# Cross-attention softmax weights: turned by VectorE in 32x32 squares and moved by transfers inside SBUF, with seven products chained in PSUM and divisions on GpSimd

## The chip, the cores and the metric

The kernel runs on one core of one Trainium2 chip. The metric is the device time of one execution in microseconds; the median of three runs of the kernel before is 2532.26 us (2529.63 to 2534.01). A core has TensorE (matmuls; PE, with its weight loads as PEld), VectorE (DVE), ScalarE (ACT), GpSimd (POOL) and SyncE (SP), each with its own in-order instruction stream, and 16 DMA engines. All data here is float32. SBUF is the working memory with 128 partitions; PSUM takes the results of TensorE, in 8 banks of 2 KB a partition.

## The reference

The reference is a cross-attention block (L0) followed by a transformer block (L1) of a diffusion model: self-attention, a second cross-attention on the same context, and an MLP. B = 8, N = 512 tokens, H = 512, 16 heads of 32, context S = 77. The change touches the two cross-attentions only. Cut to these:

```python
# L0: cross-attention with adaptive LayerNorm; lq = 512, lkv = 77
xq  = _ada_ln(x_q,  t_vec, Wss_q,  bss_q)
xkv = _ada_ln(x_kv, t_vec, Wss_kv, bss_kv)
q = (xq @ Wq + bq).reshape(B, Lq, nh, dh)
kv = (xkv @ Wkv + bkv).reshape(B, Lkv, 2, nh, dh)
scores = jnp.einsum('bqhd,bkhd->bhqk', q, k) / jnp.sqrt(jnp.float32(dh))
attn = jax.nn.softmax(scores, axis=-1)
out = jnp.einsum('bhqk,bkhd->bqhd', attn, v).reshape(B, Lq, H)
x = x_q + (out @ Wp + bp)
...
# L1, between self-attention and MLP
q_c  = _ln(x) @ W_qc + b_qc
kv_c = _ln(context) @ W_kvc + b_kvc
c_attn_w = jax.nn.softmax(jnp.einsum('bhqd,bhsd->bhqs', q_c, k_c) * scale, axis=-1)
c_attn_out = jnp.einsum('bhqs,bhsd->bhqd', c_attn_w, v_c)
x = x + (c_attn_out @ W_cproj + b_cproj)
```

## The kernel before

The program runs four phases one after another: a cross phase `x` (L0), a self-attention phase `a`, a cross phase `c`, and the MLP phase `m`. Rows of x stay in DRAM between the phases; each phase loads one batch element b at a time (`next_x`, 1 MB a load) and adds its results to the rows in DRAM by accumulating transfers on GpSimd's queue (L664).

A cross phase is `cross_phase`, run twice. Its loop has 32 steps: for every b the 16 heads go in four softmax groups fc of four heads. In the cross phases the order of the work on TensorE, VectorE, ScalarE and GpSimd is the order in which the program lists it; SyncE's order is left to a scheduler. Of one group:

- `scores` (L687): 32 matmuls, four heads by four row tiles of 128 tokens, into two PSUM tiles of two banks (`s`, two buffers, so one group's worth). Half 0 holds heads 0 and 1, half 1 heads 2 and 3.
- Half 0: VectorE takes the row maxima (L703) and writes the differences to SBUF (L704), ScalarE the exponentials in one instruction (L714). Half 1: VectorE takes the negative maxima (L710), and ScalarE computes the exponentials from PSUM in eight instructions of 77 columns with the maximum as bias (L717). VectorE sums both halves (L724), takes reciprocals (L727) and multiplies (L728). The division of half 1 is done one group later, among the next group's maxima.
- `turn` and `keep` (L741, L745): one group later, TensorE turns the weights, four 128x77 squares for each head, into a PSUM tile (tag `t`, two buffers), and ScalarE copies them to SBUF as `pT`, head by head.
- `outputs` (L751, L759): four matmuls with the values, 512 tokens wide, into a `t` tile, copied by ScalarE with the value bias to `oT`.

The order of tokens in `pT` and `oT` is plain. Between the pieces of a group stands other work (`g`, `turned`, `scaled`, `stats`):

- `Seven` (L509): the projections of 512x512 by 512x512 in seven products of half-size blocks, two halves of the output at a time. Each product is two matmuls of 256 columns. The products are written to halves of PSUM banks (tag `m`, two buffers), and their sums are formed on VectorE (L517, L520, L528, L532, and L635 or L670/L671), ScalarE (L631, L634, L659) and GpSimd (L523, L527, L660). `queries` uses it for q of the next b, `project` for the output projection of the b before. The combinations of operands that the products need are formed on GpSimd ahead: `x_sums` (L563 to L566) and `o_sums` (L556 to L559), four instructions of 128x512 each.
- `ln_rows`: LayerNorm statistics (L258, L259), the reciprocal root in small VectorE steps (L220 to L229) and the normalisation of four row tiles on ScalarE (L247). `ln_T`: the normalised rows turned by TensorE (L280) and copied by ScalarE (L284), once a b.
- `fill`: other work in fixed groups (`mod.block`, keys of the context).

Of the kernel before, what the change touches and what calls it, by code (L numbers as in the profile page):

```python
# [11 lines left out]
F32 = mybir.dt.float32  # L12
# [17 lines left out]
def tile_pixart_block(ctx: ExitStack, tc: tile.TileContext, a: dict, out: bass.AP):  # L30
# [241 lines left out]
    def ln_T(b, nm, pool, psp, res, scale=None, shift=None, tag="t"):  # L272
# [4 lines left out]
        for k in range(KC):  # L277
            pt = psp.tile([P, H], F32, tag=tag, name=f"lnT_ps_{nm}{b}_{k}")
            for t in range(NT):
                nc.tensor.transpose(pt[:, ts(t, P)], xb[:, t, ts(k, P)], ident)  # L280
            if scale is None:
                nc.scalar.copy(xT[:, k, :], pt)
            else:
                nc.scalar.activation(  # L284
                    xT[:, k, :], pt, AF.Identity,
                    bias=shift[:, k, b : b + 1], scale=scale[:, k, b : b + 1],
                )
            yield
# [49 lines left out]
    with tc.tile_pool(name="ps_s", bufs=2, space=PSUM, reuse_waits="tile") as ps_s:  # L338
# [147 lines left out]
        class Seven:  # L486
# [5 lines left out]
            ORDER = (1, 2, 6, 5, 7, 4, 3)  # L492

            def __init__(self, nm, lhs, rhs, work, first, fifth, third, dst, done=None):
                self.nm, self.lhs, self.rhs, self.work = nm, lhs, rhs, work
                self.first, self.fifth, self.third = first, fifth, third
                self.dst, self.done = dst, done

            def temp(self, tag):
                return self.work.tile([P, N2], F32, tag=tag, bufs=1 + (tag != "u3"), name=f"{tag}_{self.nm}")  # L500

            def steps(self):
                add = ALU.add
                for n, i in enumerate(self.ORDER):
                    if n % 2 == 0:
                        bank = ps_m.tile([P, 2, N2], F32, tag="m", name=f"s{n}_ps_{self.nm}")
                    ps = bank[:, n % 2]
                    for k in range(2):
                        nc.tensor.matmul(  # L509
                            ps, lhsT=self.lhs[i][:, k], rhs=self.rhs[i][:, k],  # L510
                            start=(k == 0), stop=(k == 1),
                        )

                    if i == 2:
                        p1 = self.temp("p1")
                        self.first(p1, bank[:, 0])
                        nc.vector.tensor_tensor(self.dst[0, 0], ps, p1, add)  # L517
                    elif i == 5:
                        u2, p5 = self.temp("u2"), self.temp("p5")
                        nc.vector.tensor_tensor(u2, bank[:, 0], p1, add)  # L520
                        self.fifth(p5, ps)
                        u4 = self.temp("u4")
                        nc.gpsimd.tensor_tensor(u4, u2, p5, add)  # L523
                    elif i == 4:
                        u3 = self.temp("u3")
                        self.third(u3, bank[:, 0], u2)
                        nc.gpsimd.tensor_tensor(self.dst[1, 1], u3, p5, add)  # L527
                        nc.vector.tensor_tensor(self.dst[1, 0], ps, u3, add)  # L528
                        if self.done is not None:
                            self.done(1)  # L530
                    elif i == 3:
                        nc.vector.tensor_tensor(self.dst[0, 1], ps, u4, add)  # L532
                        if self.done is not None:
                            self.done(0)
                    yield

        def cross_phase(
# [11 lines left out]
            add, sub = ALU.add, ALU.subtract  # L549

# [3 lines left out]
            def sums(engine, s1, s2, s3, s4, a11, a12, a21, a22):  # L554

                engine.tensor_tensor(s1, a21, a22, add)  # L556
                engine.tensor_tensor(s2, s1, a11, sub)
                engine.tensor_tensor(s3, a11, a21, sub)
                engine.tensor_tensor(s4, a12, s2, sub)  # L559

            def differences(engine, t1, t2, t3, t4, b11, b12, b21, b22):

                engine.tensor_tensor(t1, b12, b11, sub)  # L563
                engine.tensor_tensor(t2, b22, t1, sub)
                engine.tensor_tensor(t3, b22, b12, sub)
                engine.tensor_tensor(t4, b21, t2, sub)  # L566
# [4 lines left out]
            sums(  # L571
                nc.gpsimd, *sq,
                w_q[:, low, :H2], w_q[:, high, :H2], w_q[:, low, H2:], w_q[:, high, H2:],
            )
            to = four("to", [P, 2, H2])

            dq = small.tile([P, 2], F32, tag="dq", bufs=1, name=f"dq_{nm}")
            nc.vector.tensor_tensor(dq, bias_cols(bq, 2, 2), bias_cols(bq, 2, 0), sub)


            db = work.tile([P, H2], F32, tag="db", bufs=1, name=f"db_{nm}")
            nc.gpsimd.tensor_tensor(db, bo_row[:, H2:], bo_row[:, :H2], sub)

            def weights_o():
                differences(
                    nc.gpsimd, *to,
                    w_o[:, low, :H2], w_o[:, low, H2:], w_o[:, high, :H2], w_o[:, high, H2:],
                )

            def x_sums(b, engine):  # L590
# [4 lines left out]
                differences(  # L595
# [4 lines left out]
            def o_sums(b, engine):  # L600
# [4 lines left out]
                sums(  # L605
# [4 lines left out]
            def queries(b, j):  # L610
# [7 lines left out]
                for i in range(2):  # L618
# [8 lines left out]
                }  # L627
                return Seven(
                    f"q{nm}{b}_{j}", lhs, rhs, work,

                    lambda p1, ps: nc.scalar.activation(  # L631
                        p1, ps, AF.Identity, bias=bias_cols(bq, 1, j)
                    ),
                    lambda p5, ps: nc.scalar.copy(p5, ps),  # L634
                    lambda u3, ps, u2: nc.vector.scalar_tensor_tensor(  # L635
                        u3, ps, dq[:, j : j + 1], u2, add, add
                    ),
                    {(r, c): qT[r][:, (first, second)[c]] for r in range(2) for c in range(2)},
                ).steps()

            def project(b, j):
# [16 lines left out]
                def fifth(p5, ps):  # L658
                    nc.scalar.copy(p5, ps)  # L659
                    nc.gpsimd.tensor_tensor(p5, p5, db, add)  # L660

                def done(r):
# [6 lines left out]
                    f"o{nm}{b}_{j}", lhs, rhs, work,  # L669
                    lambda p1, ps: nc.vector.tensor_tensor(p1, ps, bo_row[:, :H2], add), fifth,  # L670
                    lambda u3, ps, u2: nc.vector.tensor_tensor(u3, ps, u2, add),  # L671
                    {(r, c): res[j + 2 * r][:, ts(c, H2)] for r in range(2) for c in range(2)}, done,
                ).steps()

            class Softmax:


                def __init__(self, b, fc):
                    self.b, self.fc, self.nm = b, fc, f"{nm}{b}_{fc}"

                def scores(self, before):
# [3 lines left out]
                    for t in range(NT):  # L685
# [12 lines left out]
                    self.p = [  # L698
                        work.tile([P, 2, NT, S], F32, tag="p", bufs=4, name=f"p_{self.nm}_{i}")
                        for i in range(2)  # L700
                    ]

                    nc.vector.tensor_reduce(self.mx[0], self.sv[0], AX.X, ALU.max)  # L703
                    nc.vector.tensor_tensor(  # L704
                        self.p[0], self.sv[0], self.mx[0].unsqueeze(3).to_broadcast([P, 2, NT, S]),
                        ALU.subtract,
                    )
                    if before:
                        before.divide(1)
                    nc.vector.tensor_reduce(self.mx[1], self.sv[1], AX.X, ALU.max, negate=True)  # L710

                def exp(self, i, r=0):
                    if i == 0:
                        nc.scalar.activation(self.p[0], self.p[0], AF.Exp)  # L714
                        return
                    for t in range(NT):
                        nc.scalar.activation(  # L717
                            self.p[i][:, r, t, :], self.sv[i][:, r, t, :], AF.Exp,
# [907 lines left out]
```

## Time and profile before

| | |
|---|---|
| median of three runs | 2532.26 us (2529.63 to 2534.01) |
| profiled execution, its span | 2534.4 us |
| cross phase x, first query products to last projections | about 75 to 449 us |
| cross phase c | about 1360 to 1720 us |
| mean granted TensorE clock | 0.988 |
| SyncE transfers of 1 MB for x, per b of a cross phase | one load, in phase x also one DRAM-to-DRAM copy |

The profiled execution's span is 2.1 us above the median of the runs and inside 0.4 us of their highest. In a line of stretches the columns are: the stretch, its length, busy us (and instructions) of PE, PEld, DVE, ACT and POOL, the granted TensorE clock as a share of full speed, the busy share of the DMA engines, and GB/s. In a line of the chain or of the timeline: start in us, length in us, engine, source line, operation or tile, and number of instructions. In a line of groups: line, engine, operation, tiles out<-in, shapes, count, then busy us and mean ns of one, then idle us of the engine just before and what ended it.

### The profile page before, as it was taken

What the parts mean: (1) busy time and instruction counts of PE and PEld (TensorE: products, weight loads), DVE (VectorE), ACT (ScalarE), POOL (GpSimd) and SP (SyncE); (2) the same over time, 40 slices, a digit from 0 to 9 for tenths busy, and PEclk for the clock granted to TensorE, in tenths of its full rate; (3) what the DMA queues carried; (4) which work ended last, traced back from release to release, by engine and by line L of the source; (5) the groups of instructions that cost most, each with busy time, mean ns of one, the idle gap of its engine ahead of it and who ended that gap; (6) DMA issues with size and microseconds to landing.
All of it is one profiled execution on the core that took longest, in us unless ns stands there. A gap on an engine that the chain in (4) does not pass through costs nothing.

```text
span 2534.4 us, 35276 instructions
## 1 busy us (share of the span) xinstructions
PE 2433.2 (96%) x13205; PEld 1561.7 (62%) x13205; DVE 1776.2 (70%) x3230; ACT 1226.2 (48%) x2083; POOL 1087.0 (43%) x982
## 2 busy tenths in 40 slices
PE   7999999889999999999989999998999999999998
PEld 3577776423333333333335777767888888888887
DVE  3588887478889888887756888877556555555553
ACT  1466665377677777777653666662121121121120
POOL 2245452266767777767663454535102102012011
PEclk9899999999999999999999999999999999999999
DMA  7323313498989999999996223133111111001010
GB/s 261 137 51 92 92 26 76 90 180 168 199 171 197 191 181 186 182 188 180 201 200 173 68 39 63 19 81 82 40 32 38 33 39 38 26 29 55 17 38 25
DMA packets 112068, 265.05 MB, mean 105 GB/s; under 512 B 12210, under 2 KB 28674, under 8 KB 111770
## 3 DMA queue, kind: packets, MB, share of 16 engines
q0 software_dynamic: 50976, 159.45, 35.1%
q1 hardware_dynamic: 54981, 91.59, 10.9%
q10 hardware_dynamic: 5941, 11.76, 1.4%
q8 instruction: 104, 1.70, 0.3%
q14 instruction: 66, 0.54, 0.1%
HBM read 226.39 MB, written 44.76 MB: 107 GB/s over the span
## 4 chain that ended last, share of the span: by engine, by line
PE 41%; issue 28%; DVE 15%; DMA 6%; POOL 6%; ACT 3%; POOLq 0%; SPq 0%; ACTq 0%; DVEq 0%
PE s_ps_qx L509 4%; PE s_ps_qc L509 4%; DMA e_a<-mxd_a 4%; DVE mx_a L1005 3%; PE proj_ps_a L301 3%; PE sT_a L985 3%; PE v_ps L301 3%; PE s_ps_ox L509 2%; PE q_ps_a L293 2%; PE s_ps_oc L509 2%; POOL res_m L1535 2%; DVE tu_a L1016 2%; DVE part_a L1017 2%; POOL xr L1536 2%; PE o_ps_a L1065 2%
## 5 line engine op out<-in xcount | busy, mean ns | idle before, releaser
L1535 POOL TENSOR_TENSOR res_m<-res_m,gate_m 128x256 f32<-128x256 f32 x64 | 52.1, 814 | 665.1 <-DVE res_m L1533 665.1
L1039 POOL DMA_DIRECT2D e_a<-mxd_a x256 | 249.8, 2045 | 157.4 <-DMA mxd_a<-mxT_a 138.6
L1048 ACT ACTIVATE e_a<-e_a 128x1024 f32<-128x1024 f32 x256 | 264.8, 1057 | 82.4 <-DMA e_a<-mxd_a 82.2
L1003 ACT COPY e_a<-sT_a 128x1024 f32<-128x1024 f32 x256 | 254.7, 1010 | 100.7 <-DVE mx_a L1005 50.5
L1469 ACT ACTIVATE hT<-hT,bcol 128x512 f32<-128x512 f32 x128 | 91.9, 721 | 237.0 <-DVE hT L1444 228.9
L1055 POOL TENSOR_TENSOR sum_a<-e_a,e_a 128x1024 f32<-128x1024 f32 x64 | 151.0, 2389 | 105.6 <-ACT e_a L1048 105.2
L1055 POOL TENSOR_TENSOR sum_a<-sum_a,e_a 128x1024 f32<-128x1024 f32 x64 | 170.7, 2678 | 3.7 <-ACT e_a L1048 3.6
L1005 DVE TENSOR_TENSOR mx_a<-sT_a,mx_a 128x1024 f32<-128x1024 f32 x128 | 150.8, 1216 | 29.7 <-PE sT_a L985 27.3
L985 PE MATMUL sT_a<-qT_a,kT_a 32*128 32x512 f32 x1024 | 151.6, 646 | 14.0 <-ACT e_a L1003 12.4
L1065 PE MATMUL o_ps_a<-e_a,v 128*32 128x512 f32 x1024 | 146.5, 613 | 9.7 <-ACT e_a L1048 9.7
L1436 PE MATMUL q_ps_h<-x_m,w_L_xcond_W_mlp 128*128 128x256 f32 x512 | 132.1, 381 | 0.0
L1436 PE MATMUL q_ps_h<-xT_m,w_L_xcond_W_mlp 128*128 128x256 f32 x512 | 131.4, 379 | 0.0
L1083 DVE RECIPROCAL rz_a<-z_ps_a 128x512 f32<-128x512 f32 x32 | 107.4, 3357 | 32.0 <-PE z_ps_a L1076 32.0
L293 PE MATMUL q_ps_a<-xnT_a,w_L_xcond_W_qkv 128*128 128x512 f32 x256 | 124.1, 613 | 5.9 <-ACT xnT_a L908 5.9
L1436 PE MATMUL q_ps_h<-x_m,w_s 128*128 128x256 f32 x512 | 122.3, 382 | 5.6 <-DVE w_s L1390 4.9
L293 PE MATMUL k_ps_a<-xnT_a,w_L_xcond_W_qkv 128*128 128x512 f32 x256 | 120.5, 608 | 0.0
L301 PE MATMUL v_ps<-w_L_xcond_W_qkv,xnT_a 128*128 128x512 f32 x256 | 119.7, 611 | 0.0
L301 PE MATMUL proj_ps_a<-w_L_xcond_W_proj,oT_a 128*128 128x512 f32 x256 | 117.9, 604 | 1.4 <-DVE oT_a L1086 1.4
L1436 PE MATMUL q_ps_y<-w_L_xcond_W_mlp,h_s 128*128 128x256 f32 x512 | 113.1, 379 | 0.0
L1436 PE MATMUL q_ps_y<-w_L_xcond_W_mlp,hT 128*128 128x256 f32 x512 | 113.1, 379 | 0.0
L1451 ACT COPY p_h<-q_ps_h 128x256 f32<-128x256 f32 x64 | 23.7, 370 | 183.7 <-PE q_ps_h L1436 183.7
L985 PEld LDWEIGHTS sT_a<-qT_a,kT_a 32*128 32x128 f32 x1024 | 42.0, 183 | 114.4 <-issue 43.4
(368 smaller groups left out, 5609.4 us busy)
## 6 DMA issues: line engine op xcount, KB each, us to landing
e_a<-mxd_a POOLq DMA_DIRECT2D x256, 512.0 KB, 11.7
xa<-res_x POOLq DMA_DIRECT2D x32, 256.0 KB, 5.4
xa<-res_a POOLq DMA_DIRECT2D x32, 256.0 KB, 14.8
x_c<-xa SPq DMA_DIRECT2D x8, 1024.0 KB
w_L_xcond_W_mlp<-in_L_xcond_W_mlp_dram SPq DMA_DIRECT2D x8, 1024.0 KB
xa<-res_c POOLq DMA_DIRECT2D x32, 256.0 KB, 5.2
x_m<-xa SPq DMA_DIRECT2D x8, 1024.0 KB
xr<-xa SPq DMA_DIRECT2D x64, 128.0 KB
```

The costliest lines, as they stand in the source:

```text
L293: nc.tensor.matmul(ps, lhsT=w[:, k, ts(j, P)], rhs=xT[k], start=(k == 0), stop=(k == KC - 1))
L301: nc.tensor.matmul(ps, lhsT=xT[k][:, cols], rhs=w[:, k, :], start=(k == 0), stop=(k == KC - 1))
L509: nc.tensor.matmul(ps, lhsT=self.lhs[i][:, k], rhs=self.rhs[i][:, k], start=(k == 0), stop=(k == 1),)
L985: nc.tensor.matmul(sc[h // 2][:, h % 2, :], lhsT=kT[ts(h, HD), ts(k, P)], rhs=qT[ts(h, HD), :], start=True, stop=True,)
L1003: nc.scalar.copy(self.e[k][i], sc[i])
L1005: nc.vector.tensor_tensor(self.mx[1 - i], sc[1 - i], self.e[0][1 - i] if k == 1 else self.mx[1 - i], ALU.max,)
L1039: nc.gpsimd.dma_start(out=self.e[k][i].rearrange("p h n -> p (h n)"), in_=self.mxd[2 * i : 2 * i + 2, :] .rearrange("h n -> (h n)").partit ...
L1048: nc.scalar.activation(self.e[k][i], self.e[k][i], AF.Exp)
L1055: engine.tensor_tensor(sum_i, self.e[0][i] if k == 1 else sum_i, self.e[k][i], ALU.add)
L1065: nc.tensor.matmul(self.po[ts(h, HD), :], lhsT=vt[:, self.fc * P + h * HD : self.fc * P + (h + 1) * HD], rhs=self.e[k][h // 2][:, h % 2, : ...
L1083: nc.vector.reciprocal(r, self.pz)
L1436: nc.tensor.matmul(self.banks[n][:, half], lhsT=lhsT, rhs=rhs, start=(k == 0), stop=(k == len(pairs) - 1),)
```

## The change

Only `cross_phase`, `Seven` and the PSUM pools change, apart from one buffer count in `ln_T`.

- The weights of a half lie in a fixed buffer `p_half[i]` of 8 blocks of 96 columns (77 and 19 zeros, set once); `pw` and `pT` have one buffer each. VectorE turns them in 32x32 squares (`turn`, one instruction a half), and twelve transfers on SyncE's queue (`send`) move rows of 2 KB between partitions: 32 partitions for each of four query squares and three key squares, 13 in the last. `pT` then holds tokens in another order, which `outputs` undoes in the view that its copy reads. The last group of a phase is still turned by TensorE (`turn_here`).
- The division of both halves runs on GpSimd. The exponentials of half 1 also sum their rows (`accum_out`), so VectorE sums half 0 only.
- The seven products of `Seven` are chained: 1, 6, 5 and 3 accumulate in one PSUM tile, read after each step (`take`); 2 in half of a second, 7 and 4 accumulate in its other half. Products 3 and 4 and what follows them are done in the next group (`pending`). The sums need three additions on VectorE; biases come in with the readings on ScalarE, or on VectorE and GpSimd for projections (`later`, `flush`).
- PSUM tag `m` gets three buffers, tag `t` one.
- `x_sums` and `o_sums` are given out in pieces; row transposes of the next b move from fc = 2 to fc = 0, queries from fc = 3, 0 to fc = 1, 3, projections to fc = 2 and 0, fills by one group or more, the load of x from fc = 3 to fc = 1.

```diff
-            ORDER = (1, 2, 6, 5, 7, 4, 3)
...
+            def mm(self, i):
+                if i == 1:
+                    self.a = ps_m.tile([P, N2], F32, tag="m", name=f"sa_ps_{self.nm}")
+                elif i == 2:
+                    self.b = ps_m.tile([P, 2, N2], F32, tag="m", name=f"sb_ps_{self.nm}")
+                if i in (2, 7):
+                    self.product(self.b[:, i == 7], i, first=True)
+                elif i == 4:
+                    self.product(self.b[:, 1], i)
+                else:
+                    self.product(self.a, i, first=(i == 1))
...
+            def add(self, dst, half, src):
+                nc.vector.tensor_tensor(dst, self.b[:, half], src, ALU.add)
...
+            p_half = [
+                work.tile([P, 2 * NT, KB * SQ], F32, tag=f"half{i}", bufs=1, name=f"p{i}_{nm}")
+                for i in range(2)
+            ]
+            for p in p_half:
+                nc.gpsimd.memset(p[:, :, S:], 0.0)
...
+                def taken(what, dst, ps):
+                    row = j if what in ("p1", "c12") else j + 2
+                    nc.scalar.activation(dst, ps, AF.Identity, bias=bias_cols(bq, 1, row))
...
+                def taken(what, dst, ps):
+                    bias = bo_row[:, H2:] if what in ("u4", "c12") else bo_row[:, :H2]
+                    if what in ("p1", "c12"):
+                        nc.vector.tensor_tensor(dst, ps, bias, add)
+                    else:
+                        nc.scalar.copy(dst, ps)
+                        later.append(lambda: nc.gpsimd.tensor_tensor(dst, dst, bias, add))
...
                     for t in range(NT):
                         nc.scalar.activation(
-                            self.p[i][:, r, t, :], self.sv[i][:, r, t, :], AF.Exp,
-                            bias=self.mx[i][:, r, t : t + 1],
+                            v[:, r, t, :], self.sv[i][:, r, t, :], AF.Exp,
+                            bias=self.mx[i][:, r, t : t + 1], accum_out=self.sm[i][:, r, t : t + 1],
                         )
...
                 def divide(self, i):
-                    nc.vector.reciprocal(self.sm, self.sm)
-                    return nc.vector.tensor_tensor(
-                        self.p[i], self.p[i], self.sm.unsqueeze(3).to_broadcast([P, 2, NT, S]), ALU.mult
+                    v = self.value(i)
+                    nc.gpsimd.tensor_tensor(
+                        v, v, self.sm[i].unsqueeze(3).to_broadcast([P, 2, NT, S]), ALU.mult
                     )
...
+                def turn(self, i):
+                    if i == 0:
+                        self.pw = work.tile([P, KB, 4, NT * SQ], F32, tag="pw", bufs=1, name=f"pw_{self.nm}")
+                    to_ = self.pw[:, :, 2 * i : 2 * i + 2, :].rearrange("p k r (t c) -> p (r t) k c", c=SQ)
+                    nc.vector.transpose(to_, self.p[i].rearrange("p g (k c) -> p g k c", c=SQ))
...
+                def send(self):
+                    self.room()
+                    for i in range(QB):
+                        for k in range(KB):
+                            n = min(SQ, S - k * SQ)
+                            nc.sync.dma_start(
+                                out=self.pT[k * SQ : k * SQ + n, i],
+                                in_=self.pw[i * SQ : i * SQ + n, k],
+                            )
```

The order inside a group becomes (whole, but for the end of a phase and the first group):

```diff
+                now.scores()
+                if before:
+                    before.turn(1)
+                    before.send()
+                if pending:
+                    pending.c22()
+                now.maxima(0)
+                now.shift()
+                now.maxima(1)
+                pump(side, 3)
+                if pending:
+                    pending.mm(3)
+                    pending.take("c12")
+                now.exp(0)
+                if pending:
+                    pending.mm(4)
+                    pending.c21()
+                    pending.stores()
+                run(tail)
+                mm(1)
+                if n:
+                    pump(turned)
+                mm(2)
+                if seven:
+                    seven.take("p1")
+                now.exp(1, 0)
+                now.total(0)
+                now.divide(0)
+                run(side)
+                if n:
+                    pump(turned)
+                mm(6)
+                if n:
+                    pump(turned)
+                mm(7)
+                if fc < 3:
+                    pump(stats)
+                if seven:
+                    seven.take("u2")
+                if n:
+                    pump(turned)
+                mm(5)
+                if seven:
+                    seven.c11()
+                now.exp(1, 1)
+                last = now.total(1)
+                now.divide(1)
+                if seven:
+                    seven.take("u4")
+                flush()
+                if fc == 2:
+                    pump(stats)
+                elif fc == 3:
+                    pump(stats, 2)
+                if n + 1 < B * KC:
+                    now.turn(0)
...
+                if before:
+                    before.outputs()
```

Here `turned` is `ln_T` of the next b (fc = 0), `tail` the last two row normalisations for it, `stats` the LayerNorm pieces of the b after, and `side` the x sums (fc = 1) or o sums (fc = 2).

## The prediction

> **What bounds the kernel now.** I read the page first, then the busy time in equal stretches of both cross phases, then the chain of waits inside one stretch, then the groups of instructions and SyncE's queue in order of time.
>
> ```profile
> PE 2433.2 (96%) x13205; PEld 1561.7 (62%) x13205; DVE 1776.2 (70%) x3230; ACT 1226.2 (48%) x2083; POOL 1087.0 (43%) x982
> ...
> 218.00:261.00 43.00, 42.36 (x354) 33.50 (x353) 37.19 (x80) 28.42 (x71) 21.27 (x22) 1.00 0.32 75
> ```
>
> The second line is one whole batch element b of the first cross phase (from 75 to 449 us; the second runs from 1360 to about 1720): TensorE is busy 42.4 of 43 us at full clock, VectorE 37.2, ScalarE 28.4, GpSimd 21.3. The chain of waits in that stretch is TensorE alone, one softmax group from its scores to the next scores:
>
> ```profile
> 259.09 1.06 PE s_x L687 x32
> 260.15 0.59 PE pT_ps_x L741 x4
> 260.74 1.73 PE s_ps_qx L509 x8
> 262.47 0.44 PE pT_ps_x L741 x4
> ...
> 263.77 0.44 PE pT_ps_x L741 x4
> ...
> 265.08 0.44 PE pT_ps_x L741 x4
> 265.51 2.59 PE s_ps_qx L509 x12
> 268.11 1.00 PE o_ps_x L751 x8
> ```
>
> The group takes 10.0 us: scores 1.06, seven products 6.04, outputs 1.0, and the four turns of weights (pT) 1.9. Scores of b = 3 start at 216.19, of b = 4 at 259.09, of b = 5 at 301.99: 42.9 us per b, three groups near 10.2 and one with the row transposes (lnT) of 12.4.
>
> **What is removed.** The four pT turns: by the timeline 0.50 + 3 x 0.44 = 1.82 us of TensorE a group, 31 groups a phase, two phases: 113 us. Were TensorE still the bound, b would fall to 42.9 - 4 x 1.82 = 35.6 us. ScalarE loses four pT copies a group (L745, 582 ns, starting some 0.49 apart), VectorE two divisions (L728, 851 ns), one sum (L724, 784 ns) and part of the additions behind the products (five or six become three for queries and five for projections, 0.41 to 0.48 each); GpSimd loses the additions L523 and L527 (0.73 each). None of these engines sets the end now.
>
> **What is added.** The rows that I price by:
>
> ```profile
> L717 ACT ACTIVATE p_x<-s_x,mx_x 128x77 f32<-128x77 f32 x256 | 61.7, 327 | 0.4
> L383 POOL TENSOR_TENSOR cT_x<-cT_x,mod_kv 128x616 f32<-128x616 f32 x4 | 4.8, 1213 | 24.6 <-DVE cT_x L379 24.6
> L1016 DVE STREAM_TRANSPOSE tu_a<-mx_a 128x512 f32<-128x512 f32 x128 | 90.7, 708 | 3.3
> ```
>
> - Two GpSimd divisions a group, same shape and broadcast as L383: 1.21 us each. Dear end: GpSimd's slope from 128x256 (725 ns) to 128x512 (1267) carried on to 616 elements, 1.49. I take L383.
> - Two VectorE turns of 768 elements: L1016's 708 ns less some 0.17 fixed (a 128x4 operation takes 0.16), over 512 elements, gives 1.05 ns an element: 0.98 us.
> - Twelve SBUF transfers on SyncE. Four loads issued in a row, and a load that waits for a store to land, show the price:
>
> ```profile
> 1733.97 1.79 SPq L1524 DMA_DIRECT2D xr<-xa  x4
> ...
> 2510.61 0.34 SPq L1537 DMA_DIRECT2D out_dram<-xr  x1
> 2512.33 0.32 SPq L1524 DMA_DIRECT2D xr<-xa  x1
> ```
>
>   Issues are (1.79 - 0.34)/3 = 0.48 us apart, and 1.72 us pass from the start of an issue to the landing. Twelve: 11 x 0.48 + 1.72 = 7.0 us. Cheap end: 0.33 each, 5.4.
> - The eight exponentials of the second half now also sum their rows, and in the changed program each waits for the one before. Today four take 0.96 us (started 0.21 apart). One after another: 0.327 + 0.04 for the hop = 0.37. No row shows the accumulator's own cost: between nothing and a small instruction such as the 128x8 reciprocal (0.20). I take 0.42, 1.7 us for four; ends 0.96 (waits free) and 2.3.
> - Reordered outputs: same element count as L751 and L759 (0.69); taken as nothing, since they run beside the exponentials' chain below; a copy twice as long would add 0.7 us to ScalarE, which is free between u4 and the next first exponential for longer than that. Two memsets of 8x19 at the start (a 128x10 one took 0.13) lie before the first group. Moved fills are the same instructions elsewhere. The products' new waits (each reading of the chained bank ends before the next product) are in the chain below; a product takes 0.87 us, a reading 0.37 to 0.47 and a hop, so one product between covers it.
>
> **The new chain.** This decides. Half buffers p, pw and pT are single, and VectorE's order is reciprocal of half 1, turn 0, turn 1 (waits for GpSimd's division), then c22 and the next maxima. Behind the waiting turn 1 stands the whole next softmax; ScalarE's exponentials wait for it. With time from the end of a turn 1, a query group (fc = 3): c22 0.34, maximum 0.83, shift 0.80, hop 0.05, first exponential 0.61, p1 0.37 (starts 0.61 and 0.37 apart, as L714 and L631 now), = 3.0; four exponentials to 4.7, u2 to 5.0, four more to 6.7; hops and reciprocal 0.4; division 1.21 to 8.3; hop and turn 1.1: **9.4 us**. Beside it: transfers landed at 7.1, outputs 8.1, next scores 9.2, just before the maximum needs them at 9.7; and the next turns, which wait for pw to be free, could end at 7.1 + 2 x 0.98 = 9.05. So TensorE (8.1 us) waits.
>
> The others, by the same rows:
> - fc = 0: after the first exponential (2.63) ScalarE does two row normalisations (L247, 1.5 for two), and its copies xnT (L284, 0.78) stand between the exponentials; tag t has one buffer, so a turn and its copy alternate. Normalised 4.2, turned 4.65, xnT0 5.4, exponentials 7.0, xnT1 7.75, turn and xnT2 9.2, u2 9.5, xnT3 10.7, exponentials 12.3, then 0.4 + 1.21 + 1.1: **15.0**.
> - fc = 1: GpSimd is later. From -1.1: two additions 1.45, three x sums 3.8, two store issues (L664, 1.04) 2.1, division 1.2, fourth sum 1.3, division 1.2, = 9.95; turn: **11.0**.
> - fc = 2: no p1 on ScalarE, exponentials end 6.4, reciprocal 6.7, then seven rsqrt steps (0.2 each, and L228 waits 0.28 longer than its neighbours, twice) to 8.7, two turns: **10.6**.
>
> Sum 46.0 a b against 42.9: +3.1. Twelve full b, and the first and last b of each phase together as two: 14 x 3.1 = 43. The closing turn, which stays on TensorE with one t buffer and a GpSimd division, adds about 1.5 a phase. 43 + 3 = 46 on the span of 2534.4, whose profiled execution lies 2.1 above the median 2532.3; 2532.3 + 46 = **2578**.
>
> [...] L383 takes 1.4 times VectorE's L728. [...] I keep the row. [...]
>
> ```profile
> 90.00:120.00 30.00, 27.83 (x160) 12.85 (x160) 21.59 (x53) 17.13 (x42) 3.16 (x4) 0.77 0.20 63
> ```
>
> Here, where TensorE waits for VectorE between groups, its granted clock is 0.77, against 1.00 in the full stretches. The chain above has it idle a fifth of the time. [...] By the row, outputs and scores at half clock end 2.06 later, 1.5 beyond their slack; in half the groups that is 3 us a b, 42 in all. I take none and keep it as the dear end.
>
> **Rivals.**
> - Cheap ends: accumulators free (0.96), issues 0.33. fc = 3 then 8.2 (TensorE), fc = 0 13.5, fc = 1 stays 11.0 on GpSimd, fc = 2 9.1: 41.8, so 14 x -1.1 + 3 = -12: 2520. For it: the exponentials run 0.21 apart today. Against: the added waits. 0.13.
> - TensorE stays the bound everywhere: -113 + 3: 2422. For it: 98% busy now. Against: fc = 0 and the single buffers. 0.07.
> - Dear ends: accumulators 0.57 apart (+1.2 a group where ScalarE leads), divisions 1.49 (+0.27, twice in fc = 1): 16.5 + 11.5 + 12.1 + 10.9 = 51.0: +8.1 x 14 + 3 = +116: 2648; or the clock, +42 on the forecast. 0.20.
> - A load ahead of the transfers on SyncE (a 1 MB load and a 1 MB copy keep DMA busy 5 us from 204 to 209 us): landing at 12.1, turns at 14 for 11.0 in fc = 1: +3 for 7 b, 21. It lies inside the range; the load waits for lnT3 (about 10) and should be through before turn 1 at 15.
>
> **How the numbers follow.** Forecast 0.60 at 2578, its own range 2545 to 2615. What a measurement can tell is 0.2%, 5 us. Faster: 0.07 and 0.11 of the cheap case, 0.18; same: the rest of it and a sliver of the forecast, 0.05; slower 0.77. The range leaves out the TensorE case and the upper part of the dear one: 2515 to 2645.
>
> **What would show it.** The changed profile should have TensorE near 80% busy in the cross stretches at 46 us per b; exponentials 0.4 apart, not 0.21; GpSimd divisions near 1.2 us; VectorE idle before turn 1 on GpSimd; the fc = 0 group near 15 us. I am wrong if TensorE is still 95% busy there, if accumulating exponentials overlap, or if turn 0 waits on DMA for longer than turn 1 on GpSimd.

## The result and the profile after

The changed kernel takes 2791.22 us (median of 4 runs, 2785.63 to 2794.27), the kernel before 2533.14 in the same comparison: ratio 1.1015, 95% interval 1.0992 to 1.1037. It is slower by 258 us where I forecast slower by 46. The profiled execution has a span of 2787.3 us. First the line of busy time of the changed kernel's page, then its busy time in one stretch of 58 us, which is one b of the first cross phase (columns as in the stretch shown of before: length, TensorE, weight loads, VectorE, ScalarE, GpSimd, granted clock, DMA share, GB/s):

```profile
PE 2470.7 (89%) x12213; PEld 1542.4 (55%) x12213; DVE 1734.7 (62%) x3064; ACT 1193.3 (43%) x2443; POOL 1162.9 (42%) x1016
```

```profile
376.00:434.00 58.00, 45.48 (x300) 32.53 (x300) 35.40 (x70) 26.02 (x93) 25.86 (x24) 0.82 0.31 62
```

A b takes about 58 us, not 42.9 and not the 46.0 of my sum. No engine is full: TensorE is busy 45 of 58, and that at a granted clock of 0.82. So the time is in waits, and in work that runs at a lower clock behind them. The order of time of one group, from the end of a turn to the end of the next, shows which (changed kernel; start, length, engine, instruction, in brackets the idle time before it and what ended it). The first line is SyncE's first send of the group, the next two its third and its last:

```profile
391.54 0.51 SPq L806 DMA_DIRECT2D pT_x<-pw_x  x1
...
392.74 0.80 SPq L806 DMA_DIRECT2D pT_x<-pw_x  x1
...
399.03 1.03 SPq L806 DMA_DIRECT2D pT_x<-pw_x  x1
...
403.05 1.84 DVE L795 STREAM_TRANSPOSE pw_x<-p_x 128x768 f32<-128x768 f32 x2 [4.67 <-DMA pT_x<-pw_x]
403.08 1.94 PE L828 MATMUL o_ps_x<-pT_x,cv_x 77*32 77x512 f32 x8 [4.95 <-DMA pT_x<-pw_x]
404.95 2.01 PE L741 MATMUL s_x<-ckT_x,qT_x 32*128 32x77 f32 x32
...
406.99 0.80 DVE L760 TENSOR_REDUCE mx_x<-s_x 128x8 f32<-128x616 f32 x1 [1.80 <-PE s_x L741]
```

This is a group fc = 1. From the first send to the landing of the last pass 11.5 us, where I had 7.0. VectorE's next turns and TensorE's outputs both wait for that, and the scores stand behind the outputs. TensorE, 4.95 us idle, runs outputs and scores at half speed (1.94 and 2.01 us, against 1.07 and 1.13 when it comes straight from other work), so that the next maximum starts 15.5 us after the first send. My sum had it wanted at 9.7 in a group fc = 3, and by the same steps at some 11.3 in a group fc = 1 (11.0 and the addition c22, 0.34). In the first phase VectorE's turns wait for the landing in 13 of 31 groups, 37.2 us in all, in the second in 16, 48.5 us.

Group by group, from the end of one turn 1 to that of the next (in the changed kernel SyncE's first send marks it, 0.07 to 0.18 behind), beside the run without transfers, which is the first experiment:

| group | prediction | changed kernel | without transfers |
|---|---|---|---|
| fc = 0 | 15.0 | 14.85 | 14.00 |
| fc = 1 | 11.0 | 13.53 | 10.55 |
| fc = 2 | 10.6 | 16.63 | 12.25 |
| fc = 3 | 9.4 | 12.87 | 11.28 |
| a b | 46.0 | 57.9 | 48.1 |

(Sends at 376.69, 391.54, 405.07, 421.70, 434.57; turn ends without transfers at 282.61, 296.61, 307.16, 319.41, 330.69.)

In this b the turns and outputs of fc = 1 and fc = 3 wait for the landing. The group that grows most, fc = 2, does not; it pays for the wait before it. First three lines of the changed kernel, then the same product and sum without transfers:

```profile
408.75 1.92 PE L501 MATMUL sb_ps_qx<-xs_x,w_L_xcond_Wq 128*128 128x256 f32 x4
...
410.70 0.42 DVE L527 TENSOR_TENSOR qT_x<-sb_ps_qx,u_qx 128x256 f32<-128x256 f32 x1 [1.38 <-PE sb_ps_qx L501]
...
412.18 0.78 DVE L781 TENSOR_REDUCE sm_x<-p_x 128x8 f32<-128x616 f32 x1
```

```profile
307.61 1.10 PE L501 MATMUL sb_ps_qx<-xs_x,w_L_xcond_Wq 128*128 128x256 f32 x4 [1.22 <-DVE qT_x L527]
...
310.29 0.78 DVE L783 TENSOR_REDUCE sm_x<-p_x 128x8 f32<-128x616 f32 x1
```

From the end of the turn to the first maximum pass 2.1 us against 0.2, as the scores are late; to the sum it is 7.3 against 3.1, as the products between run at half speed (granted clock 0.50 from 403 to 411) and VectorE waits for them. These 4.2 us are nearly all of the 4.4 that the group grows.

### The profile page after: what moved, and what is told of

Same layout as the page of the kernel before. It is cut to its first block, busy times and chain, and to the rows that moved or that the text cites. A ratio compares the mean times of both kernels' runs of the same rounds, so it can differ in the third digit from the quotient of the medians.

```text
span 2787.3 us, 34823 instructions
## 1 busy us (share of the span) xinstructions
PE 2470.7 (89%) x12213; PEld 1542.4 (55%) x12213; DVE 1734.7 (62%) x3064; ACT 1193.3 (43%) x2443; POOL 1162.9 (42%) x1016
## 5 line engine op out<-in xcount | busy, mean ns | idle before, releaser
L786 POOL TENSOR_TENSOR p_x<-p_x,sm_x 128x616 f32<-128x616 f32 x64 | 89.7, 1410 | 226.5 <-DVE sm_x L782 151.1
L786 POOL TENSOR_TENSOR p_c<-p_c,sm_c 128x616 f32<-128x616 f32 x64 | 88.7, 1387 | 212.5 <-DVE sm_c L782 116.9
```

What stands on the lines that cost most here:

```text
L786: nc.gpsimd.tensor_tensor(v, v, self.sm[i].unsqueeze(3).to_broadcast([P, 2, NT, S]), ALU.mult)
```

## The experiments

Theory, after reading the traces: the twelve sends and what waits for their landing make a second loop beside the chain that I summed, and it is the longer one. Rivals: the divisions on GpSimd; the accumulating exponentials; the single buffer that the turns wait for; the bytes moved. Every run was timed against the kernel before on the same chip; its median moved between 2533.7 and 2537.0.

| run | us | ratio to before, 95% interval |
|---|---|---|
| no transfers (left out) | 2623.25 | 1.0325 to 1.0366 |
| TensorE turns | 2783.46 | 1.0957 to 1.0994 |
| divisions on VectorE | 2778.93 | 1.0940 to 1.0977 |
| no accumulation | 2801.67 | 1.1026 to 1.1070 |
| two queues, 6 + 6 | 2759.23 | 1.0872 to 1.0905 |
| pw double | 2778.04 | 1.0944 to 1.0994 |
| 32 rows each | 2776.26 | 1.0936 to 1.0969 |
| chain opened, two queues | 3011.38 | 1.1864 to 1.1903 |
| a quarter of the bytes | 2752.03 | 1.0836 to 1.0909 |
| six of twelve sends | 2629.06 | 1.0348 to 1.0381 |
| chain opened, no transfers | 2596.55 | 1.0226 to 1.0260 |
| chain opened, SyncE alone | 2942.04 | 1.1585 to 1.1624 |
| nine + three | 2744.40 | 1.0799 to 1.0864 |
| nine + three, VectorE divides | 2735.91 | 1.0756 to 1.0823 |
| stores late | 2747.36 | 1.0815 to 1.0866 |
| nine + three, stores late | 2651.12 | 1.0433 to 1.0485 |

**Without transfers.** `send` only takes the tile; one constant `pT` serves all outputs.

```diff
-                    for i in range(QB):
-                        for k in range(KB):
...
+            nc.gpsimd.memset(pT_one, 1.0 / S)
```

> Left out: the twelve transfers of every group; the outputs read a constant tile instead of the turned weights. All the rest of the change stays. Theory: the 14.9 us that a b has gained (57.9 against 42.9) hang on the loop through SyncE (turn, twelve issues of 8.1 us, landing some 2.5 us after the last one, next turns of 1.9): without it the chain that I summed at 46 us a b is left, 2560 to 2620 us. Rival (the chain itself: GpSimd's divisions and what they do to VectorE, or the accumulating exponentials): most of the time stays, above 2720. Rival (TensorE's clock): follows the idle, so it goes with whichever cause is true.

```profile
282.60:330.70 48.10, 40.60 (x291) 28.37 (x289) 34.60 (x71) 26.14 (x92) 25.95 (x24) 0.93 0.39 110
```

2623.25: 168 of the 258 us hang on the transfers, and a b falls to some 48 (the line is one, with columns as above). What remains, 88 us, is the chain and the ends of the phases. The theory holds (3 us above the end of its range).

**Turns back on TensorE.**

```diff
-                    before.turn(1)
-                    before.send()
...
                 mm(1)
+                if before:
+                    before.turn_here([0])
```

> Undone alone: the 32x32 squares and the transfers. TensorE turns the weights of every group among the products (two buffers of p for that, one PSUM bank for all turns), ScalarE copies them; divisions on GpSimd, accumulating exponentials and chained products stay. Theory: 2520 to 2620, as TensorE has 43 us of work a b again and the loop through SyncE is gone. Rival (divisions on GpSimd or accumulating exponentials set the time): above 2720.

2783.46, which by my wording speaks for the rival. But it is no clean undo, as the order of time in its trace shows:

```profile
325.89 0.66 PE L280 MATMUL lnT_ps_x<-ident,x_x 128*128 128x128 f32 x4 [0.67 <-ACT pT_x L817]
...
326.95 0.78 ACT L284 ACTIVATE xnT_x<-lnT_ps_x,mod_q 128x512 f32<-128x512 f32 x1
327.87 0.63 PE L816 MATMUL pT_ps_x<-ident,p_x 128*77 128x128 f32 x4 [0.46 <-ACT xnT_x L284]
```

Turns, row transposes and outputs now share one PSUM bank (tag t), and each waits until ScalarE has copied the one before, between exponentials. A b takes 57.2 us, for reasons of its own. That the second bank would mend this was not tried; the run decides nothing between theory and rival.

**Divisions on VectorE, and no accumulation.**

```diff
-                    nc.gpsimd.tensor_tensor(
+                    nc.vector.tensor_tensor(
                         v, v, self.sm[i].unsqueeze(3).to_broadcast([P, 2, NT, S]), ALU.mult
```

> Undone alone: the divisions, back on VectorE. Theory: the loop through SyncE stays, 12.4 us a group; what goes is the wait of the turns in fc = 2 behind the rsqrt steps, which stand still while GpSimd works (about 4 us of 17.5 in one group of four): 57.9 to about 54 a b, 2700 to 2770 us. Rival (divisions are the cause): below 2620.

```diff
-                            bias=self.mx[i][:, r, t : t + 1], accum_out=self.sm[i][:, r, t : t + 1],
+                            bias=self.mx[i][:, r, t : t + 1],
```

> Undone alone: the row sums in the exponentials of half 1; VectorE sums them again (0.78 us a group). Theory: within 15 us of the changed kernel, 2775 to 2805, as neither engine sets the end of a group. Rival (accumulating exponentials are the cause): below 2700.

2778.93 and 2801.67. Neither rival, undone alone, takes the loss away. The first gains 12 us where I expected 20 or more. VectorE's own divisions take 0.80 us where nothing gets in their way, but in most b one meets GpSimd's stores and sums in fc = 1 and lasts 4.28 us (the mean of the first phase is 1.16):

```profile
398.79 4.28 DVE L786 TENSOR_TENSOR p_x<-p_x,sm_x 128x616 f32<-128x616 f32 x1
```

How much of the missing gain that is was not measured. The second loses 10, as expected.

**Two queues, six sends each.**

```diff
-                            nc.sync.dma_start(
+                            (nc.sync, nc.scalar)[i // 2].dma_start(
```

> Six of the twelve transfers of a group are issued by ScalarE, six by SyncE; all else as in the changed kernel. Theory (issues in a row on one queue are the long term of the loop): if ScalarE issues at SyncE's pace, the row of issues falls from 8.1 to 4.1 us and the loop from 12.9 to 8.8, so that the chain without transfers (48 us a b) and up to 2 us a group that ScalarE loses before its first exponential are left: 48 to 54 a b, 2625 to 2710 us. Rival (the landing, that is the bytes or the 16 engines, is the long term): above 2750.

2759.23, above the theory's range, where the rival was to be. In order of time in its trace:

```profile
365.96 4.27 ACTq L806 DMA_DIRECT2D pT_x<-pw_x  x6
...
370.28 0.72 ACT L771 ACTIVATE p_x<-p_x 128x616 f32<-128x616 f32 x1 [9.43 <-DMA pT_x<-pw_x]
...
374.37 1.06 PE L828 MATMUL o_ps_x<-pT_x,cv_x 77*32 77x512 f32 x8
374.69 1.23 POOL L786 TENSOR_TENSOR p_x<-p_x,sm_x 128x616 f32<-128x616 f32 x1 [1.26 <-DVE sm_x L782]
```

The outputs no longer wait for a transfer. But ScalarE issues for 4.27 us, and its first exponential, ready when the shift ends at 367.8, starts at 370.28: 2.5 us are put into the chain instead. So the rival's number came by another way.

**A quarter of the bytes, and half of the sends.** These part the count of sends from what they carry; what is left out is read from a constant tile. In the first each send carries one head in place of four; in the second the loop over query blocks stops half way.

```diff
-                                out=self.pT[k * SQ : k * SQ + n, i],
-                                in_=self.pw[i * SQ : i * SQ + n, k],
+                                out=self.pT[k * SQ : k * SQ + n, i, 0],
+                                in_=self.pw[i * SQ : i * SQ + n, k, 0],
```

> Left out: three quarters of what each transfer carries (one head in place of four, 512 bytes a row in place of 2048); the other heads are read from a constant tile. Still twelve transfers on SyncE. Theory (issues in a row set the loop): the issues stay where they were, 8.1 us a group, and only the landing gets somewhat shorter: 2740 to 2795 us. Rival (bytes, or the 16 engines): close to the kernel without transfers (2623), below 2680.

```diff
-                    for i in range(QB):
+                    for i in range(QB // 2):
```

> Left out: six of the twelve transfers of a group (two of the four blocks of queries are read from a constant tile); the other six stay on SyncE with all their bytes. Theory: the row of issues falls to some 4 us, the loop to 8.9, below the chain without transfers (48 us a b), without the six issues that ScalarE got in the run with two queues: 2625 to 2690 us. Rival (a fixed price of waiting for any transfer): above 2720.

2752.03 and 2629.06: both as the theory had it. With a quarter of the bytes the first send and the outputs behind the last one stand here:

```profile
381.43 0.51 SPq L808 DMA_DIRECT2D pT_x<-pw_x  x1
...
389.29 0.80 SPq L808 DMA_DIRECT2D pT_x<-pw_x  x1
...
393.08 1.93 PE L830 MATMUL o_ps_x<-pT_x,cv_x 77*32 77x512 f32 x8 [3.85 <-DMA pT_x<-pw_x]
```

11.65 us again, with 0.56 to 0.95 us from one issue to the next. The bytes of the sends do not set it; a quarter of them gains 39 us. With six sends the loop drops below the chain, and the time is within 6 us of no transfers at all. What TensorE's outputs waited for the landing in the first phase (us, times), in the changed kernel and with six sends:

```profile
  DMA pT_x<-pw_x: 50.1, 15
```

```profile
  DMA pT_x<-pw_x: 0.7, 1
```

**Two buffers for pw, and 32 rows in every send.**

```diff
-                        self.pw = work.tile([P, KB, 4, NT * SQ], F32, tag="pw", bufs=1, name=f"pw_{self.nm}")
+                        self.pw = work.tile([P, KB, 4, NT * SQ], F32, tag="pw", bufs=2, name=f"pw_{self.nm}")
```

> Two buffers for the turned squares (pw), so that the next turns no longer wait for the transfers to land; all else as in the changed kernel. Theory: the issues stay in a row and the outputs still stand before the next scores on TensorE; only the turns (1.9 us) leave the loop and the outputs (1.0) enter it, 1 us a group at most: 54 to 57 a b, 2735 to 2785 us. Rival (the single buffer that the turns wait for is the cause, not the issues): below 2700.

```diff
-                    self.pT = work.tile([S, QB, 4, NT * SQ], F32, tag="pT", bufs=1, name=f"pT_{self.nm}")
+                    self.pT = work.tile([KB * SQ, QB, 4, NT * SQ], F32, tag="pT", bufs=1, name=f"pT_{self.nm}")
...
-                            n = min(SQ, S - k * SQ)
+                            n = SQ
```

> The four transfers of 13 rows become transfers of 32 rows (the padding goes along): more bytes, the same count. In the changed kernel the three of a row take 0.52, 0.59 and 0.80 us to issue, the last being the one of 13 rows. If the 13 rows make it dear: some 0.25 us less for each, 1 us a group off the loop, 2735 to 2780. If its place does, or the bytes count: no gain, 2785 to 2810.

2778.04 and 2776.26, both in range: the single buffer is not the cause, and the rows are a small part. Three issues in a row with 32 rows each, of the second run:

```profile
374.79 0.51 SPq L806 DMA_DIRECT2D pT_x<-pw_x  x1
375.35 0.58 SPq L806 DMA_DIRECT2D pT_x<-pw_x  x1
375.98 0.58 SPq L806 DMA_DIRECT2D pT_x<-pw_x  x1
```

The third, 0.80 with 13 rows in the changed kernel, takes 0.58 with 32: fewer rows made it dearer.

**The chain opened.** VectorE's order puts turn 1 ahead of the next maxima. Here half 1 and pw have two buffers and the turn goes behind them (p1 loses a buffer for room): once with 6 + 6 sends, once without transfers, once with all sends on SyncE (of 32 rows).

```diff
-                if before:
-                    before.turn(1)
-                    before.send()
...
                 now.maxima(1)
+                if before:
+                    before.turn(1)
+                    before.send()
```

> Both loops opened: transfers on two queues, two buffers for pw, two for half 1 of the weights, and the turn of half 1 moved behind the next maxima and shift on VectorE (p1 has one buffer, to make room). Theory: neither the loop through SyncE (8.8 us) nor the chain of VectorE's order (48 a b) is closed any more; what is left is busy time, TensorE 36 to 40 us a b and VectorE about 37, and the group with the row transposes: 42 to 48 a b, 2520 to 2625 us. Rival (VectorE and GpSimd holding each other up, or ScalarE's issues): above 2650.

> Left out: all transfers, as in the run without them. Besides, the chain through VectorE's order is opened: two buffers for half 1 and for pw, the turn of half 1 behind the next maxima and shift. Theory: what is left of the loss without transfers (88 us) is mostly the closed chain from turn to turn: 40 to 45 a b, 2500 to 2580. Rival (the readings of the chained products between the exponentials on ScalarE, and VectorE held up by GpSimd): within 20 us of 2623.

> All of the computation, all transfers on SyncE with 32 rows each; the chain opened as in the run with two queues and the late turn, but without ScalarE's issues. Theory: issues 7.5, landing 2.4, outputs 1.0 and a wait or two: 11 to 12.5 us a group, 2590 to 2700 us. Rival (the loss of that run, 3011, came from the late turn and not from ScalarE's issues): above 2790.

3011.38, 2596.55 and 2942.04. My theory failed on the first and the third, and missed the second by 17 us. The order of time of the third shows why (outputs, scores, the next maximum, the late turn):

```profile
322.56 1.94 PE L828 MATMUL o_ps_x<-pT_x,cv_x 77*32 77x512 f32 x8 [5.16 <-DMA pT_x<-pw_x]
324.43 2.01 PE L741 MATMUL s_x<-ckT_x,qT_x 32*128 32x77 f32 x32
326.47 0.80 DVE L760 TENSOR_REDUCE mx_x<-s_x 128x8 f32<-128x616 f32 x1 [7.30 <-PE s_x L741]
...
328.72 0.97 DVE L795 STREAM_TRANSPOSE pw_x<-p_x 128x768 f32<-128x768 f32 x1
```

The turn now waits for the maxima, these for the scores, these for the outputs, and these for the landing of the group before: I had opened one loop and closed a longer one, some 16.6 us a group (322.56 to 339.14 from outputs to outputs). Without transfers the opened chain gains 27 us over the closed one, in between what theory and rival had said. So the chain through VectorE's order is part of the 88 us, and not most of it.

**Nine sends on SyncE, three on ScalarE.** All of 32 rows; the second run divides on VectorE besides.

```diff
-                            nc.sync.dma_start(
+                            (nc.sync, nc.scalar)[i // 3].dma_start(
```

> All of the computation; all transfers with 32 rows; nine on SyncE, three on ScalarE. Theory (the row of issues sets the loop, and the run with two queues gained little because ScalarE's six issues, 4.3 us, stand before its first exponential, which is ready some 2.3 us after the turn): SyncE's row is 8 x 0.63 = 5.0 us, the landing 3.4, the turns 1.9, a hop: 10.4 a group, below the 12 of the chain; ScalarE's three issues (1.9 us) are over when the exponential is ready. 48 to 51 a b: 2625 to 2700 us. Rival (issues on ScalarE cost in any number, or two queues slow each other): above 2735.

> As the run with nine and three, and the divisions back on VectorE. Once the loop is out of the way, the chain shows what the division on GpSimd costs: VectorE needs 0.85 in place of 1.2 and two hops, and the rsqrt steps are no longer held up by it (1.12 in place of 0.17 us for one). Theory: 1 to 3 us a b below the run with nine and three, 15 to 45 us faster. Rival (VectorE, with 5 us a b more to do, becomes the bound): equal or slower.

2744.40 and 2735.91. The first misses its theory by 44 us: the sends last 10.3 us from first to landing even so (383.55 to 393.81 in its trace). The second gains 8 us, half of the least I expected, and the two intervals overlap; what the division on GpSimd costs stays small and not well measured. For the first, the mean busy share of the 16 DMA engines shows what held the landing up. The window is 14 us in 40 slices of 0.35, each digit a tenth; first the changed kernel from 391 on (a group with two stores of 256 KB, issued by GpSimd), then the changed kernel from 376 on (a group without), then nine and three from 383 on (with):

```profile
DMA  0000162504251603096999998899852100000000
```

```profile
DMA  0000061703071603162603253412000000000010
```

```profile
DMA  0000278889362254397989999989630000000002
```

Alone, each send is a short burst, and traffic ends 1.8 us after the last issue's start (384.01 to 385.8). With stores the engines are full from the 18th slice or so on, and traffic ends 3.2 us after it (399.03 to 402.2); with nine and three it ends at 393.9 although the last issue started at 389.08.

**The stores moved.** `pending.stores()` goes from behind `c21` to just ahead of `now.turn(0)`: GpSimd issues them behind the second division.

```diff
                     pending.c21()
-                    pending.stores()
...
+                if pending:
+                    pending.stores()
                 if n + 1 < B * KC:
                     now.turn(0)
```

> The changed kernel with one move: the two stores of a group (512 KB, in the groups fc = 1 and fc = 3) are issued on GpSimd behind the second division, not ahead of the first. All twelve transfers as they were. In the changed kernel the engines' traffic of such a group ends some 1.8 us after the last issue, filled by the stores, where it ends 1.0 after it in a group without stores. Theory (the stores hold the last transfers up, on top of the row of issues): 1 us in two groups of four, and GpSimd's divisions 1.8 us earlier in them: 2 to 4 us a b, 2735 to 2765 us. Rival (the stores do not matter to the landing): within 10 us of 2791.

> Nine transfers on SyncE, three on ScalarE, all of 32 rows, and the stores behind the second division. In the run with nine and three without this, landing in fc = 1 came 4.1 us after the last issue's end, with the engines full of store traffic from 5 us after the first issue on; without stores it should come some 2.2 after it. Theory: 2 us off the landing in two groups of four, and what stands behind it (outputs, scores, the next maxima, all at half clock) with it: 3 to 6 us a b against 2744: 2660 to 2705 us. Rival (a second queue itself is slow to land): 2730 or more.

2747.36 and 2651.12, the first in its range, the second 9 us below. Each mending alone gains 44 to 47 us, both together 140. A group with stores in the last run (stores, next turns, outputs):

```profile
313.88 1.76 POOL L713 DMA_DIRECT2D xa<-res_x  x2
315.04 1.84 DVE L795 STREAM_TRANSPOSE pw_x<-p_x 128x768 f32<-128x768 f32 x2 [2.40 <-DMA pT_x<-pw_x]
315.07 1.07 PE L828 MATMUL o_ps_x<-pT_x,cv_x 77*32 77x512 f32 x8 [2.67 <-DMA pT_x<-pw_x]
```

From the first send (305.76) to the landing 9.3 us, with a pause of 1.75 on SyncE in it, and outputs at full speed. This is the fastest version with all of the computation; it is still 4.3 to 4.9% slower than the kernel before. Nothing tried beats the kernel before.

## Why the prediction was wrong

- **The failed step** is "Twelve SBUF transfers on SyncE", 0.48 apart and 1.72 to landing, 7.0 us in all, with the sentence built on it, that landing, outputs and scores end "just before the maximum needs them". Measured in the b shown: 7.3 to 7.7 us from the first issue's start to the last one's (0.56, 0.63 and 0.85 from one to the next, in place of 0.48), and 3.3 to 4.0 us to the landing in groups with stores. Together 11 to 11.5. Without stores beside it the loop is too long as well. First send, last send and outputs of such a group in the second phase:

```profile
1569.02 0.52 SPq L806 DMA_DIRECT2D pT_c<-pw_c  x1
...
1576.38 0.80 SPq L806 DMA_DIRECT2D pT_c<-pw_c  x1
...
1578.63 1.94 PE L828 MATMUL o_ps_c<-pT_c,cv_c 77*32 77x512 f32 x8 [2.44 <-DMA pT_c<-pw_c]
```

  That is 9.6 us, 2.25 of them from the last issue to the landing. So of the 4.0 to 4.5 us above my 7.0, the issues are 2.2 to 2.4, a quiet landing 0.5, the stores 1.0 to 1.8. My price for the issue came from loads of 128 KB out of DRAM, the one for the landing from a queue with nothing beside it. With 7.0 the loop lay 0.35 us under the chain; it was the term with the least slack, and I had put no dear end on its price. Only the cheap end, 5.4, was in the range, and a late landing behind a load of x. That one did not come: in the cross phases of the changed kernel every load on SyncE is issued behind the last send of a group.
- **What it cost.** Leaving the sends out gives 168 us back, leaving half of them out 162; sending nine on SyncE and three on ScalarE, all of 32 rows, with the stores out of the way gives 140. That the wait passes from the landing through outputs and scores to the next softmax is read in the trace of the changed kernel, and the run with the late turn (2942) shows what the loop does when more is hung into it. Listing the next scores ahead of the outputs on TensorE, which would part these two, was not tried.
- **The clock**, taken as no loss, which no row of before shows, was one. TensorE's granted clock is 0.82 in the stretch, and after a wait of 4.95 us outputs and scores took 0.87 and 0.88 us more; after waits of 2.24 and 2.35 the outputs kept 1.07. In the last run one output ran at half speed after 2.66 us and another at full speed after 2.67; in the changed kernel one ran at half speed after 2.44 us (1578.63), and one at full speed after 4.29 (543.11), with the product behind it at half. So the length of a wait alone does not tell the speed of the work behind it. The half clock of my dear end stands in the trace of before, in the stretch from 90 to 120 us that I had weighed: from 105 to 110 us the granted clock is 0.52, and 28 of the 32 matmuls of a group's scores take 1.97 us (105.15), where all 32 take 1.06 at full clock. As fc = 2 shows, not only outputs and scores pay. I should not have taken it as nothing, but the clock follows the waits: without transfers the stretch has 0.93. What the clock alone costs was not measured.
- **The chain was nearly right.** Summed 46.0 us a b, measured 48.1 without transfers. fc = 0: 15.0 against 14.00, fc = 1: 11.0 against 10.55. fc = 2 came out 1.65 dearer and fc = 3 1.9. In fc = 2 rsqrt steps on VectorE take longer: one of them (L225) took 1.12 us in the median over the first phase without transfers, 0.17 at the least; I had allowed 0.28 us, twice.
- **Single prices held**, but for the division. It took 1.22 to 1.25 us where nothing got in its way (taken 1.21), but up to 1.90 beside other work: its mean, 1.41 and 1.39 in the two phases, lies nearer my dear end of 1.49. The turn took 0.93 to 0.98 (taken 0.98). Accumulating exponentials start 0.30 apart, not 0.42: each is followed by a separate reading of 0.21 us. Groups of the changed kernel (280 to 520 us; the division over the whole first phase):

```profile
L774 ACT ACTIVATE p_x<-s_x,mx_x 128x77 f32<-128x77 f32 x135 | 41.8, 329 | 0.0
L774 ACT ACTIVATION_READ_ACCUMULATOR p_x<-s_x,mx_x 128x1 f32 x135 | 28.5, 211 | 0.0
...
L786 POOL TENSOR_TENSOR p_x<-p_x,sm_x 128x616 f32<-128x616 f32 x64 | 89.7, 1410 | 226.5 <-DVE sm_x L782 151.1
```

- **The ends** of the phases, priced at 3 us, are dearer. Without transfers the stretches from first to last scores grow by 37.6 and 25.8 us (336.6 to 374.2, 332.5 to 358.3), 63 of the 88, where I had 43; some 24 lie outside them, 11 of these between the last scores of the self-attention and the first scores of the second cross phase (85.6 to 96.6). That part was not tried by itself and stays open.
- **The rivals.** TensorE as the bound (2422) and the cheap ends (2520) fell. The dear ends reached 2648 by exponentials, which were not dear, and divisions, which in part were; undoing either moved the time by 10 to 12 us. What came was the last item on my own list, the turn 0 that waits on DMA: it waits 37 us in the first phase, and turn 1 for GpSimd's division 1.7.

## What to carry to other kernels

The transfers that replaced an instruction here cost their issues as serial time of one queue (7.3 to 7.7 us from the first of twelve to the last) and their landing as latency (2.25 us from the start of the last issue in a group without stores, 3.3 to 4.0 in groups with); count both with rows of the same kind of transfer, and look for other queues' traffic at that moment. If its result stands ahead of other work in an engine's order (here outputs ahead of scores, which started 13.4 us after the first send), a late landing delays all of that, and a second loop has to be summed, with a dear end, even where it seems to fit under the first. Issues moved to a second queue held up what that engine had waiting behind them: ScalarE's first exponential, by 2.5 us.

## What the runs showed of the hardware

- A send of 13 rows took 0.80 us to issue in most cases, one of 32 rows 0.51 to 0.60, with more bytes.
- The time from first send to landing was 11.5 us with 2048 bytes a row and 11.65 with 512, both in a group with stores.
- Stores issued by GpSimd delayed the landing of SyncE's transfers: from the start of the last issue to the landing it was 3.3 to 4.0 us in groups with stores and 2.25 in a group without. Nine and three without moving the stores gained a third of what they gained with (47 against 140 us), and from first send to landing it was 10.3 us without and 9.3 with. From the first issue's start to the last one's it was 7.5 of the 11.5 us in the group shown of the changed kernel.
- One VectorE operation of 128x4 elements took 1.12 us in the changed kernel and 0.17 with the divisions on VectorE (280 to 520 us):

```profile
L225 DVE TENSOR_SCALAR lnv_x<-lnv_x 128x4 f32<-128x4 f32 x3 | 3.4, 1119 | 0.1
```

```profile
L225 DVE TENSOR_SCALAR lnv_x<-lnv_x 128x4 f32<-128x4 f32 x3 | 0.5, 171 | 0.1
```

  The step of 1.12 us starts 0.13 after a division and ends with it (413.47 to 414.59 beside 413.34 to 414.56). What holds it up, no run here shows.
